# Two attention blocks on one core: row-sum reciprocals taken in 128x8 form through DRAM, one range watch at the end, and VectorE in place of GpSimd for the scaling

## The chip, the cores and the metric

The kernel runs on one core of one Trainium2 chip. A core has a matrix engine (TensorE, PE in the profile), a vector engine (VectorE, DVE), an activation engine (ScalarE, ACT), a general engine (GpSimd, POOL) and a queue engine (SyncE, SP) that here only issues DMAs. Each works through its own instructions in order and waits on semaphores for the others. The metric is the device time of one execution in microseconds; lower is better. Three runs of the kernel before took 2831.9, 2832.25 and 2833.12 us: median 2832.25 us.

## The reference

The input x is eight images (B = 8) of 512 channels by 32x32 = 1024 tokens, in f32. Two attention blocks follow one another:

```python
# layer 0: 8 heads of 64 channels, GroupNorm(32)
h = group_norm(x); q, k, v = per head (w_qkv @ h + b_qkv)
weight = softmax(q.k / sqrt(64), over s);  a = weight @ v
x = x + w_proj @ a + b_proj
# layer 1: one head of 512 channels, GroupNorm(8)
xn = group_norm(x); attn = softmax(q.k / sqrt(512)); out = attn @ v
x = x + p_w @ out + p_b
```

Softmax is a row of exponentials divided by its sum. This kernel takes the exponentials without subtracting a maximum and multiplies the finished product by the reciprocal of each sum. So that this is safe, it keeps a watch over all reciprocals: if one is outside 1e-20 to 1e20, a slow general path recomputes everything at the end. With the inputs here the general path does not run.

## The kernel before, in words

The outer loop goes over the images, b = 0 to 7. In each turn the layer-0 attention of image b is followed by its output projection, then by the layer-1 scores, z product and values of image b-1, then by the layer-0 v, k and q products of the next image. The products are Strassen-Winograd forms ("wino", "conv2", "inner_steps"), which put sums and differences on VectorE and GpSimd.

**A stretch.** `attention0` (L617) goes through 8 stretches per image: 4 pairs of heads, times 2 halves of the 1024 tokens. In a stretch TensorE makes the scores of 8 token blocks (`sc`), ScalarE takes their exponentials (L635, 128x1024 each), and VectorE adds the 8 results into `total` (L637 once, L639 six times). TensorE then multiplies the exponentials by v (`av`), and at once, in `reciprocals` (L588), forms the row sums from `total` with a matrix of ones: 4 products into a PSUM tile `sums`, 128x256, in which each sum stands 32 times. Then TensorE begins the scores of the next stretch. ScalarE copies `av` out to `a` (L653).

**The reciprocals.** VectorE takes the reciprocal of the whole 128x256 `sums` from PSUM (L599), keeps a running minimum (`low_recs`, L600), and GpSimd a running sum (`all_recs`, L601). Four partitions of the result go to DRAM as 4 KB (`rows`, L603) and are read back broadcast over the partitions as `r` (L613 in layer 0, 2 reads of 128 KB; L608 in layer 1, 2 reads of 256 KB). In layer 0, GpSimd multiplies `a` by `r` (L658) for 7 of 8 stretches; in the last one VectorE does, at a later place (L660), and the DMAs go by ScalarE's queue in place of SP's. Layer 1 calls `reciprocals` once per image, in a hook near the end of the z product, and `values1` (L757, L760) multiplies by `r`. In all there are 72 calls: 64 in layer 0 and 8 in layer 1.

**What sets the order.** TensorE's instructions are pinned in program order (L66 to L70). The others are placed by a list scheduler, which works with its own estimates when it builds the program: an instruction takes its place in its engine's queue when the scheduler believes its inputs to be there, the earlier one in the program first. On the chip the queue runs in that fixed order. `keep_in_program_order` pins an instruction behind the one traced just before it on its engine. `extra` is a list of small pieces of work (weight sums, image sums, GroupNorm of the next layer) that is emptied before and after the `av` products of each stretch, and most of its VectorE pieces are pinned (L1045, L285, L286). Each attention needs `a` of its last two stretches in the image sums that open the projection (`steps`, `image_factors`). The loads of x for the projection are issued during the last stretch (L209).

**Buffers.** Large tiles share a pool of 32 (`big`), `sums` and `av` share two PSUM banks (`acc`), `rc` and `r` have two buffers each.

**The end.** After the last image, L1113 reduces `low_recs` and `all_recs` over their columns, L1114 compares with the limits, L1116 multiplies the two answers, a 1x1 product counts over the partitions, and L1119 writes the flag that every engine loads before the branch to the general path.

Of the kernel before, what the change touches and what calls it, by code (L numbers as in the profile page):

```python
# [9 lines left out]
F32 = mybir.dt.float32  # L10
I32 = mybir.dt.int32
AF = mybir.ActivationFunctionType
ALU = mybir.AluOpType
AX = mybir.AxisListType

P = 128
# [6 lines left out]
RECIPROCALS_MIN, RECIPROCALS_MAX = 1e-20, 1e20  # L23
# [6 lines left out]
def two_attention_blocks_kernel(  # L30
# [8 lines left out]
    nc = tc.nc  # L39
    B, C, T = x.shape  # L40
    KC = C // P
# [3 lines left out]
    const = ctx.enter_context(tc.tile_pool(name="const", bufs=1))  # L45
    small = ctx.enter_context(tc.tile_pool(name="small", bufs=3))
# [9 lines left out]
    nc.vector.memset(ones, 1.0)  # L56
    mhalf = const.tile([P, KC], F32, name="mhalf")
    nc.vector.memset(mhalf, -0.5)

    low_recs = const.tile([P, 2, P], F32, name="low_recs")  # L60
    nc.vector.memset(low_recs, 1.0)
    all_recs = const.tile([P, 2, P], F32, name="all_recs")
    nc.gpsimd.memset(all_recs, 0.0)


    def matmul(*args, **kw):  # L66
        tc.keep_in_program_order(nc.tensor.matmul(*args, **kw))  # L67
# [16 lines left out]
    dram = ctx.enter_context(tc.tile_pool(name="dram", bufs=1, space=bass.MemoryType.DRAM))  # L84
# [91 lines left out]
    def main_path(ctx):  # L176
# [2 lines left out]
        upool = ctx.enter_context(tc.tile_pool(name="upool", bufs=1))  # L179
        rpool = ctx.enter_context(tc.tile_pool(name="rpool", bufs=2))  # L180
        rowpool = ctx.enter_context(tc.tile_pool(name="rows", bufs=3, space=bass.MemoryType.DRAM))
        spool = ctx.enter_context(tc.tile_pool(name="spill", bufs=2, space=bass.MemoryType.DRAM))
        ps_acc = ctx.enter_context(tc.tile_pool(name="ps_acc", bufs=2, space=bass.MemoryType.PSUM))

        def big_tile(name, shape=(P, T)):
            return big.tile(list(shape), F32, tag="big", name=name)

        def pair_tile(name):
            return big_tile(name, (P, 2, HT))

        def acc_tile(name):
            return ps_acc.tile([P, HT], F32, tag="acc", name=name)
# [392 lines left out]
            return out  # L585


        def reciprocals(total, uid, across, queue=nc.sync):  # L588

            sums = acc_tile(f"sums_{uid}")[:, : 2 * P].rearrange("p (a b) -> p a b", a=2)
            for i in range(4):
                matmul(sums[ts(i, 32), :, :], ones[:, :32], total[:, :, ts(i, P)], start=True, stop=True)
            rc = rpool.tile([P, 2, P], F32, tag="rc", name=f"rc_{uid}")
            nc.vector.reciprocal(rc, sums)  # L599
            nc.vector.tensor_tensor(low_recs, low_recs, rc, ALU.min)  # L600
            nc.gpsimd.tensor_tensor(all_recs, all_recs, rc, ALU.add)  # L601
            rows = rowpool.tile([2, 4, P], F32, tag="rows", name=f"rows_{uid}")
            queue.dma_start(rows.rearrange("j i n -> i j n"), rc[0:P:32, :, :])  # L603
            if across:
                r = pair_tile(f"r_{uid}")
                for j in range(2):
                    row = rows[j : j + 1].rearrange("j i n -> j (i n)")
                    queue.dma_start(r[:, j, :], row.to_broadcast([P, HT]))  # L608
            else:
                r = rpool.tile([P, HT], F32, tag="r", name=f"r_{uid}")  # L610
                for j in range(2):
                    row = rows[j : j + 1].rearrange("j i n -> j (i n)")
                    queue.dma_start(r[ts(j, 64), :], row.to_broadcast([64, HT]))  # L613
            return r


        def attention0(b, q, k, v, a, extra):  # L617
            n = 0

            for hp in range(KC):  # L620
                for tb in (0, 1) if hp < KC - 1 else (1, 0):
                    uid = f"0_{b}_{hp}_{tb}"
                    total = pair_tile(f"sum_{uid}")
                    es = []
                    for s in range(NS):

                        sc = ps_pools[(0, 2, 1)[n % 3]].tile([P, 2, HT], F32, tag="sc", name=f"sc_{uid}_{s}")
                        n += 1
                        for j in range(2):
                            matmul(  # L630
                                sc[:, j, :], k[hp][ts(j, 64), ts(s, P)], q[hp][ts(j, 64), ts(tb, HT)],
                                start=True, stop=True,
                            )
                        e = pair_tile(f"e_{uid}_{s}")
                        nc.scalar.activation(e, sc, AF.Exp, scale=(C // 8) ** -0.5)  # L635
                        if s == 1:
                            nc.vector.tensor_add(total, es[0], e)  # L637
                        elif s > 1:
                            nc.vector.tensor_add(total, total, e)  # L639
                        es.append(e)  # L640
                    for f in extra.pop(0) if extra else ():
                        f()
                    av = acc_tile(f"av_{uid}")
                    for s in range(NS):
                        for j in range(2):
                            matmul(
                                av[ts(j, 64), :], v(s, 2 * hp + j),
                                es[s][:, j, :], start=(s == 0), stop=(s == NS - 1),
                            )
                    for f in extra.pop(0) if extra else ():  # L650
                        f()
                    dst = a[hp][:, ts(tb, HT)]
                    nc.scalar.copy(dst, av)  # L653

                    last = (hp, tb) == (KC - 1, 0)
                    r = reciprocals(total, uid, False, nc.scalar if last else nc.sync)
                    if not last:
                        nc.gpsimd.tensor_tensor(dst, dst, r, ALU.mult)  # L658
                    else:
                        scaled = lambda dst=dst, r=r: tc.keep_in_program_order(nc.vector.tensor_mul(dst, dst, r))  # L660

            assert not extra
            return scaled


        def scores1(f, gf, gsteps, first, uid, stats):
# [362 lines left out]
        for b in range(B):  # L1029
            extra = [[] for _ in range(2 * 2 * KC)]  # L1030
# [17 lines left out]
            if b > 0:  # L1048
                hf, t = image_factors(h, f"h1_{b - 1}", here)
                for i, fs in enumerate((t[:1], t[1:2], (t[2], t[4]), (t[6], t[3]), (t[5], t[7]), steps[:2], steps[2:4])):  # L1050
                    extra[2 * i + 3] += fs
            elif B > 1:
                hf, t = image_factors(h, "h0_1", here)
# [3 lines left out]
            scaled = attention0(b, q, k, v, a, extra)  # L1057
# [47 lines left out]
        finish()  # L1105


        good = small.tile([P, 2], F32, tag="good", name="good")
        for i, (t, op, limit, within) in enumerate(
            ((low_recs, ALU.min, RECIPROCALS_MIN, ALU.is_ge), (all_recs, ALU.add, RECIPROCALS_MAX, ALU.is_le))  # L1110
        ):
            extreme = small.tile([P, 1], F32, tag="extreme", name=f"extreme{i}")
            nc.vector.tensor_reduce(extreme, t, AX.XY, op)  # L1113
            nc.vector.tensor_scalar(good[:, i : i + 1], extreme, limit, None, within)  # L1114
        both = small.tile([P, 1], F32, tag="both", name="both")
        nc.vector.tensor_mul(both, good[:, 0:1], good[:, 1:2])  # L1116
# [184 lines left out]
```

## Time and profile before

| What | Value |
|---|---|
| median of three runs | 2832.25 us |
| the profiled execution | 2831.03 us, of which its span is 2829.2 us |
| granted TensorE clock | 0.999 |
| TensorE, VectorE, ScalarE, GpSimd busy | 2811.2, 2119.0, 942.7, 1250.6 us |
| reciprocal, 128x256 (L599) | 72 times, mean 1756 ns |
| running minimum (L600), running sum (L601) | 72 times each, mean 438 and 887 ns |
| scaling on GpSimd (L658), on VectorE (L660) | 56 times, mean 2051 ns; 8 times, mean 682 ns |
| sum of exponentials (L639) | 384 times, mean 1351 ns |
| copy `a` (L653), 128x512 | 64 times, mean 585 ns |

One execution was recorded by the hardware profiler. Its page gives the busy time of each engine, the chain of waits that ended last, and groups of instructions. A timeline lists instructions in order of time, several of a kind merged into one row: start, time in us, engine, line, operation, output and inputs, count, and in brackets how long the engine stood idle before it and what ended the wait. "SPq" rows are DMAs being issued by SyncE's queue. The views of waits say, for each engine, what it waited for, in total.

### The profile page before, as it was taken

What the parts mean: (1) busy time and instruction counts of PE and PEld (TensorE: products, weight loads), DVE (VectorE), ACT (ScalarE), POOL (GpSimd) and SP (SyncE); (2) the same over time, 40 slices, a digit from 0 to 9 for tenths busy, and PEclk for the clock granted to TensorE, in tenths of its full rate; (3) what the DMA queues carried; (4) which work ended last, traced back from release to release, by engine and by line L of the source; (5) the groups of instructions that cost most, each with busy time, mean ns of one, the idle gap of its engine ahead of it and who ended that gap; (6) DMA issues with size and microseconds to landing.
All of it is one profiled execution on the core that took longest, in us unless ns stands there. A gap on an engine that the chain in (4) does not pass through costs nothing.

```text
span 2829.2 us, 33980 instructions
## 1 busy us (share of the span) xinstructions
PE 2811.2 (99%) x12434; PEld 1691.7 (60%) x12434; DVE 2119.0 (75%) x2877; ACT 942.7 (33%) x1205; POOL 1250.6 (44%) x1249
## 2 busy tenths in 40 slices
PE   9999999999999999999999999999999999999998
PEld 5435635866367653677537674376843868338584
DVE  5588687766877778777787667877678776887765
ACT  1252452214522145221552215422154312633130
POOL 2214215842267421674117731277223772147672
PEclk9999999999999999999999999999999999999999
DMA  8634403043031330323212232123311224112301
GB/s 286 210 114 147 151 19 121 26 178 138 20 139 53 146 129 23 131 99 119 110 49 105 101 141 90 49 102 123 139 70 49 102 112 158 35 53 95 119 5 68
DMA packets 98850, 291.68 MB, mean 103 GB/s; under 512 B 10803, under 2 KB 42867, under 8 KB 88950
## 3 DMA queue, kind: packets, MB, share of 16 engines
q1 hardware_dynamic: 96886, 287.16, 28.3%
q10 hardware_dynamic: 1792, 2.29, 0.3%
q8 instruction: 100, 1.64, 0.2%
q14 instruction: 72, 0.59, 0.1%
HBM read 236.94 MB, written 52.47 MB: 102 GB/s over the span
## 4 chain that ended last, share of the span: by engine, by line
PE 97%; DVE 1%; issue 1%; POOL 0%; ACT 0%; DVEq 0%; POOLq 0%
PE sc L67 16%; PE av L67 16%; PE psb_av L67 6%; PE psb L67 5%; PE psa_av L67 4%; PE psc_av L67 4%; PE psc L67 3%; PE psa L67 3%; PE psb_z L67 3%; PE psb_p L67 3%; PE psb_k L67 3%; PE psb_g L67 3%; PE psb_v L67 3%; PE psb_q L67 2%; PE psa_p L67 2%; PE psa_z L67 2%
## 5 line engine op out<-in xcount | busy, mean ns | idle before, releaser
L639 DVE TENSOR_TENSOR sum<-sum,e 128x1024 f32<-128x1024 f32 x384 | 518.9, 1351 | 40.7 <-ACT e L635 0.9
L635 ACT ACTIVATE e<-sc 128x1024 f32<-128x1024 f32 x512 | 476.0, 1054 | 79.1 <-PE sc L67 79.1
L67 PE MATMUL sc<-q,k 64*128 64x512 f32 x2048 | 456.8, 596 | 0.0
L67 PE MATMUL av<-e,v 128*64 128x512 f32 x2048 | 453.6, 595 | 0.0
L67 PEld LDWEIGHTS sc<-q,k 64*128 64x128 f32 x2048 | 191.6, 186 | 238.5 <-ACT e L635 109.2
L67 PEld LDWEIGHTS av<-e,v 128*64 128x64 f32 x2048 | 141.4, 137 | 304.3 <-issue 304.3
L601 POOL TENSOR_TENSOR all_recs<-all_recs,rc 128x256 f32<-128x256 f32 x72 | 63.8, 887 | 541.3 <-DVE rc L599 541.3
L658 POOL TENSOR_TENSOR a<-a,r 128x512 f32<-128x512 f32 x56 | 114.9, 2051 | 261.7 <-DMA r<-rows 245.5
L599 DVE RECIPROCAL rc<-sums 128x256 f32<-128x256 f32 x72 | 126.5, 1756 | 46.7 <-PE sums L67 25.3
L653 ACT COPY a<-av 128x512 f32<-128x512 f32 x64 | 37.4, 585 | 321.9 <-PE av L67 321.9
L637 DVE TENSOR_TENSOR sum<-e,e 128x1024 f32<-128x1024 f32 x64 | 78.8, 1231 | 57.0 <-ACT e L635 57.0
L67 PE MATMUL psb<-inner,inner_h 128*128 128x256 f32 x448 | 116.1, 382 | 0.8
L67 PE MATMUL psa_av<-e,z 128*128 128x512 f32 x256 | 113.3, 595 | 0.0
L416 POOL TENSOR_TENSOR inner_h<-h,inner_h 128x256 f32<-128x256 f32 x120 | 107.5, 897 | 3.4
L140 ACT ACTIVATE h<-h,b,s 128x1024 f32<-128x1024 f32 x62 | 78.5, 1270 | 88.0 <-DMA h<-in_x 70.4
L67 PEld LDWEIGHTS psb<-inner,inner_h 128*128 128x128 f32 x448 | 83.9, 190 | 16.6 <-POOL inner L431 3.5
L464 ACT COPY psb_v<-psa_v 128x512 f32<-128x512 f32 (+1 forms) x28 | 14.5, 517 | 227.0 <-DVE o L759 144.6
L416 POOL TENSOR_TENSOR inner_h<-h 128x256 f32<-128x256 f32 x60 | 55.6, 926 | 77.4 <-ACT h L140 77.4
L699 POOL TENSOR_TENSOR sum<-sum,e 128x1024 f32<-128x1024 f32 x32 | 76.1, 2378 | 27.1 <-ACT e L695 25.9
L67 PE MATMUL psb_g<-inner_h,w_m 128*128 128x256 f32 x336 | 85.9, 383 | 0.3
L685 DVE TENSOR_TENSOR e<-psc,u 128x512 f32<-128x512 f32 x56 | 38.7, 691 | 59.0 <-PE psc L67 58.6
L537 POOL TENSOR_TENSOR v<-v,v 128x256 f32<-128x256 f32 x28 | 20.0, 726 | 141.8 <-DVE u_v L532 141.8
(361 smaller groups left out, 5749.6 us busy)
## 6 DMA issues: line engine op xcount, KB each, us to landing
x<-in_x SPq DMA_DIRECT2D x36, 512.0 KB
h<-in_x SPq DMA_DIRECT2D x32, 512.0 KB
spill<-x SPq DMA_DIRECT2D x32, 512.0 KB
h<-spill SPq DMA_DIRECT2D x32, 512.0 KB
x<-spill SPq DMA_DIRECT2D x32, 512.0 KB
out<-x SPq DMA_DIRECT2D x64, 256.0 KB
w_p<-sums_p SPq DMA_DIRECT2D x8, 1792.0 KB
r<-rows SPq DMA_DIRECT2D x112, 128.0 KB
```

The costliest lines, as they stand in the source:

```text
L67: tc.keep_in_program_order(nc.tensor.matmul(*args, **kw))
L140: tc.keep_in_program_order(nc.scalar.activation(dst, src, AF.Identity, bias=b, scale=s))
L416: pin(nc.gpsimd.tensor_tensor(dst, x, y, ALU.subtract))
L599: nc.vector.reciprocal(rc, sums)
L601: nc.gpsimd.tensor_tensor(all_recs, all_recs, rc, ALU.add)
L635: nc.scalar.activation(e, sc, AF.Exp, scale=(C // 8) ** -0.5)
L637: nc.vector.tensor_add(total, es[0], e)
L639: nc.vector.tensor_add(total, total, e)
L653: nc.scalar.copy(dst, av)
L658: nc.gpsimd.tensor_tensor(dst, dst, r, ALU.mult)
L685: nc.vector.tensor_add(dst[0], ps, x[0])
L699: on = lambda dst, x, y: lambda: tc.keep_in_program_order(nc.gpsimd.tensor_tensor(dst, x, y, ALU.add))
```

## The change

- The two running accumulators `low_recs` and `all_recs`, with their 72 updates each on VectorE and GpSimd, are gone.
- In 64 of the 72 calls (7 of 8 stretches, and layer 1) ScalarE copies `sums` to SBUF (`line`); the raw sums go to DRAM (4 KB), come back as a 128x8 tile (`cols`), VectorE takes the reciprocal of that tile, the result goes to DRAM again, into the call's own place in `all_rows`, and from there the broadcast read goes on as before. In the 8 calls of the last stretches (`direct`) VectorE takes the reciprocal of the 128x256 tile as before.
- GpSimd's multiplication is gone. VectorE scales each stretch one stretch later, after the `av` products of the next, ahead of the pieces in `extra`, pinned behind what was traced before it on VectorE.
- At the end all 72 x 1024 reciprocals are loaded as one tile of 128x576, and the two reductions run over it.

```diff
-        def reciprocals(total, uid, across, queue=nc.sync):
+        def reciprocals(total, uid, across, direct=False):
...
-            rc = rpool.tile([P, 2, P], F32, tag="rc", name=f"rc_{uid}")
-            nc.vector.reciprocal(rc, sums)
-            nc.vector.tensor_tensor(low_recs, low_recs, rc, ALU.min)
-            nc.gpsimd.tensor_tensor(all_recs, all_recs, rc, ALU.add)
-            rows = rowpool.tile([2, 4, P], F32, tag="rows", name=f"rows_{uid}")
-            queue.dma_start(rows.rearrange("j i n -> i j n"), rc[0:P:32, :, :])
+            rows = all_rows[len(taken)]
+            taken.append(uid)
+            line = rpool.tile([P, 2, P], F32, tag="line", name=f"line_{uid}")
+            queue = nc.scalar if direct else nc.sync
+            if direct:
+                nc.vector.reciprocal(line, sums)
+                queue.dma_start(rows.rearrange("j i n -> i j n"), line[0:P:32, :, :])
+            else:
+                nc.scalar.copy(line, sums)
+                raw_rows = rowpool.tile([2, 4, P], F32, tag="rows", name=f"rows_{uid}")
+                queue.dma_start(raw_rows.rearrange("j i n -> i j n"), line[0:P:32, :, :])
+                cols = small.tile([P, 8], F32, tag="cols", name=f"cols_{uid}")
+                flat = lambda t: t.rearrange("j i n -> (j i n)").rearrange("(p m) -> p m", p=P)
+                queue.dma_start(cols, flat(raw_rows))
+                recs = small.tile([P, 8], F32, tag="recs", name=f"recs_{uid}")
+                nc.vector.reciprocal(recs, cols)
+                queue.dma_start(flat(rows), recs)
...
-                    for f in extra.pop(0) if extra else ():
+                    for f in [*scaled, *(extra.pop(0) if extra else ())]:
                         f()
                     dst = a[hp][:, ts(tb, HT)]
                     nc.scalar.copy(dst, av)
 
-                    last = (hp, tb) == (KC - 1, 0)
-                    r = reciprocals(total, uid, False, nc.scalar if last else nc.sync)
-                    if not last:
-                        nc.gpsimd.tensor_tensor(dst, dst, r, ALU.mult)
-                    else:
-                        scaled = lambda dst=dst, r=r: tc.keep_in_program_order(nc.vector.tensor_mul(dst, dst, r))
+                    r = reciprocals(total, uid, False, (hp, tb) == (KC - 1, 0))
+                    scaled = [lambda dst=dst, r=r: tc.keep_in_program_order(nc.vector.tensor_mul(dst, dst, r))]
...
+        every = big_tile("every_row", (P, stretches * 8))
+        nc.sync.dma_start(every, all_rows.rearrange("s j i n -> (s j i n)").rearrange("(p m) -> p m", p=P))
         good = small.tile([P, 2], F32, tag="good", name="good")
-        for i, (t, op, limit, within) in enumerate(
-            ((low_recs, ALU.min, RECIPROCALS_MIN, ALU.is_ge), (all_recs, ALU.add, RECIPROCALS_MAX, ALU.is_le))
+        for i, (op, limit, within) in enumerate(
+            ((ALU.min, RECIPROCALS_MIN, ALU.is_ge), (ALU.add, RECIPROCALS_MAX, ALU.is_le))
         ):
             extreme = small.tile([P, 1], F32, tag="extreme", name=f"extreme{i}")
-            nc.vector.tensor_reduce(extreme, t, AX.XY, op)
+            nc.vector.tensor_reduce(extreme, every, AX.X, op)
```

More of the change, by code (lines that the diff above doesn't have):

```diff
@@ L58, in two_attention_blocks_kernel @@
     nc.vector.memset(mhalf, -0.5)
[L60 to L63, printed above, removed]
     def matmul(*args, **kw):
@@ L181, in main_path @@
         rowpool = ctx.enter_context(tc.tile_pool(name="rows", bufs=3, space=bass.MemoryType.DRAM))
+        stretches = B * (2 * KC + 1)
+        all_rows = dram.tile([stretches, 2, 4, P], F32, name="all_rows")
+        taken = []
         spool = ctx.enter_context(tc.tile_pool(name="spill", bufs=2, space=bass.MemoryType.DRAM))
@@ L618, in attention0 @@
             n = 0
+            scaled = []
             for hp in range(KC):
@@ L653, in attention0 @@
                     nc.scalar.copy(dst, av)
-                    last = (hp, tb) == (KC - 1, 0)
-                    r = reciprocals(total, uid, False, nc.scalar if last else nc.sync)
-                    if not last:
-                        nc.gpsimd.tensor_tensor(dst, dst, r, ALU.mult)
-                    else:
-                        scaled = lambda dst=dst, r=r: tc.keep_in_program_order(nc.vector.tensor_mul(dst, dst, r))
+                    r = reciprocals(total, uid, False, (hp, tb) == (KC - 1, 0))
+                    scaled = [lambda dst=dst, r=r: tc.keep_in_program_order(nc.vector.tensor_mul(dst, dst, r))]
             assert not extra
-            return scaled
+            return scaled[0]
         def scores1(f, gf, gsteps, first, uid, stats):
@@ L1105, in main_path @@
         finish()
+        assert len(taken) == stretches
+        every = big_tile("every_row", (P, stretches * 8))
+        nc.sync.dma_start(every, all_rows.rearrange("s j i n -> (s j i n)").rearrange("(p m) -> p m", p=P))
         good = small.tile([P, 2], F32, tag="good", name="good")
-        for i, (t, op, limit, within) in enumerate(
-            ((low_recs, ALU.min, RECIPROCALS_MIN, ALU.is_ge), (all_recs, ALU.add, RECIPROCALS_MAX, ALU.is_le))
+        for i, (op, limit, within) in enumerate(
+            ((ALU.min, RECIPROCALS_MIN, ALU.is_ge), (ALU.add, RECIPROCALS_MAX, ALU.is_le))
         ):
             extreme = small.tile([P, 1], F32, tag="extreme", name=f"extreme{i}")
-            nc.vector.tensor_reduce(extreme, t, AX.XY, op)
+            nc.vector.tensor_reduce(extreme, every, AX.X, op)
             nc.vector.tensor_scalar(good[:, i : i + 1], extreme, limit, None, within)
```

## The prediction

> **What bounds the kernel now.** I read the page first: the busy shares, then the chain of waits that ended last.
>
> ```profile
> PE 2811.2 (99%) x12434; PEld 1691.7 (60%) x12434; DVE 2119.0 (75%) x2877; ACT 942.7 (33%) x1205; POOL 1250.6 (44%) x1249
> PE 97%; DVE 1%; issue 1%; POOL 0%; ACT 0%; DVEq 0%; POOLq 0%
> ```
>
> TensorE is busy 99% of the span, and the chain runs 97% through it. A busy PE need not be a PE at its peak, so I went on to what TensorE waited for in the whole span. All its waits there add up to 8.7 us; the two longest are the load of a weight at the start and one ScalarE copy:
>
> ```profile
> PE tr_wk L70 <- DMA rawk<-in_w: 3.7, 1, 3.7
> PE psb_v L67 <- ACT u_v L454: 1.2, 1, 1.2
> ```
>
> [...]
>
> The change touches VectorE, GpSimd and ScalarE, so it can win at most these 8.7 us, and little of that lies where it works. What it can lose is read from one stretch. These are rows of the timeline from 386 to 404 us, engine by engine:
>
> ```profile
> 388.15 0.64 PE L67 MATMUL sums<-sum,ones 128*32 128x256 f32 x8
> 402.80 0.64 PE L67 MATMUL sums<-sum,ones 128*32 128x256 f32 x8
> 388.91 1.76 DVE L599 RECIPROCAL rc<-sums 128x256 f32<-128x256 f32 x1 [0.40 <-issue]
> 391.86 1.22 DVE L637 TENSOR_TENSOR sum<-e,e 128x1024 f32<-128x1024 f32 x1 [0.74 <-ACT e L635]
> 393.19 8.75 DVE L639 TENSOR_TENSOR sum<-sum,e 128x1024 f32<-128x1024 f32 x6
> 388.26 0.59 ACT L653 COPY a<-av 128x512 f32<-128x512 f32 x1 [4.48 <-PE av L67]
> 389.89 7.44 ACT L635 ACTIVATE e<-sc 128x1024 f32<-128x1024 f32 x8 [1.04 <-PE sc L67]
> 396.02 2.19 POOL L658 TENSOR_TENSOR a<-a,r 128x512 f32<-128x512 f32 x1 [4.30 <-DMA r<-rows]
> 390.69 0.56 SPq L603 DMA_DIRECT2D rows<-rc  x1
> 392.40 1.10 SPq L613 DMA_DIRECT2D r<-rows  x2
> ```
>
> TensorE needs `total` at 402.80; VectorE's seven sums run from 391.86 to 401.94. So the place that decides has 0.86 us to spare, and the sums start when ScalarE has two exponentials, not when the reciprocal is done: VectorE stands idle 0.74 us before them. A faster reciprocal moves nothing here.
>
> **Part 1, VectorE's and GpSimd's work.** Gone: 64 of the 72 reciprocals at 1.76 us, 72 minima at 0.44, on GpSimd 72 sums at 0.89 (63.8 us) and 56 scalings at 2.05 (114.9). New on VectorE: 56 scalings at 0.68 (the row of L660, same shape) and 64 reciprocals of 128x8. No row has that shape; it lies between 0.06 (1756 ns by 8/256 columns) and 0.20 (the aggregation of 128x12), and I take 0.15, near the 128x4 copy. VectorE: -112.6 - 31.5 + 38.1 + 9.6 = -96 us. GpSimd's scaling also stretches one VectorE sum beside it: six sums take 8.75 here, but 7.87 in the row at 138.57, where no scaling runs beside them. So each stretch gains another 0.88, and the slack at 402.80 becomes 0.86 + 0.88 = 1.74 us. On the path: 0, since TensorE waits for none of this.
>
> **Part 2, ScalarE's copy.** 64 copies of 128x256 out of PSUM, 0.36 each (the 128x256 form of L464 has a mean of 357 ns). In the stretch it follows the copy of `a`: 388.85 to 389.21. Queued behind it are the eight exponentials; the first starts at 389.89, when its scores are there, so 0.68 us cover it. Without that cover a delay would go into the chain of sums, which has 1.74. Path: 0.
>
> **Part 3, the two extra trips, and the wait they put into VectorE's queue.** SP issues 2 more DMAs per call; on its queue they stand ahead of the next loads. The write of 4 KB takes 1.71 us (390.69 to 392.40, where the read that waits for it is issued). The raw sums go out at 389.2 and land at 390.9. The read into 128x8 has no row: from below it is a write of the same 4 KB, 1.71; from above one of the two reads of 128 KB, which take 3.62 together (392.40 to 396.02), less half of the 1.10 they take to issue, 3.07. I take 1.71, the row of the same size; `cols` is there at 392.65, at most at 394.0.
>
> The new reciprocal waits for it in VectorE's queue, with the sums of the next stretch behind it, and behind those TensorE's `sums`. If the scheduler puts it behind the first or second sum (ending 393.1 and 394.5), it costs its 0.15. If it stands ahead of the first, the sums shift by 392.65 + 0.15 - 391.86 = 0.94, still inside 1.74. At the upper bound the shift is 2.28 and TensorE loses 0.54 per stretch. Path, by the value taken: 0.
>
> The rest follows: written back by 394.65 + 1.71 = 396.4, `r` broadcast by 400.0. The scaling stands behind the sums, which now end at 401.06: 1.1 us early, and it may be 3 us late before the next sums, which cannot begin until 406.5.
>
> [...]
>
> **Part 4, the first attention, where the queues are full.** In the first two stretches the write took 4.38 and 7.06 us and `r` came 8.5 and 6.8 us after its issue:
>
> ```profile
> 134.41 0.33 SPq L291 DMA_DIRECT2D sums_p<-prepare_p  x1
> 136.20 0.61 SPq L603 DMA_DIRECT2D rows<-rc  x1
> 140.16 0.33 SPq L333 DMA_DIRECT2D w_p<-sums_p  x1
> 140.58 1.62 SPq L613 DMA_DIRECT2D r<-rows  x2
> ```
>
> They stand behind 1.8 MB stores and loads of weights. There only GpSimd waited; now VectorE will. The raw sums land at about 140.2, behind `sums_p`. If `cols` is issued ahead of `w_p`, it is there at 141.9; if behind, at about 147 (the two `r` reads behind it served GpSimd at 149.08). With the reciprocal behind the second sum (139.9) and five sums of 1.33 after it, the sums end at 148.7 or 153.8; TensorE wants them at 148.2. Loss 0.5 or 5.6, and 0 if the reciprocal stands behind all the sums. The second stretch could pay as much again: 0 to 11 in all. No row tells which order SP gets; I take the middle of 0.5 and 5.6, **3 us**, once.
>
> **Part 5, ends of attentions, layer 1, end of the kernel.** The seventh stretch's `r` now comes about 4 us later, while 2 MB of x are issued at 437.65. They are drained by 446 (410 GB/s from 442 to 444 us, 18 after 446); behind them `r` lands near 450 (446 + 3.6) instead of 441. Then follow scaling and two image sums on VectorE, 2.0 us, to 452; TensorE wants them at 454.30. Path 0, but only 2 us of cover, in each of 8 attentions. In layer 1 the sums are formed at 2766.07 and VectorE first uses `r` at 2784.08; before, the reciprocal waited until 2768.37 for its turn. The steps (0.4 + 1.7 + at most 3.1 + 0.2 + 1.7, and some 4 for `r` with twice the bytes) make 11 us and fit. At the end the load of all reciprocals (295 KB) can go when SP is idle (2774.9 to 2785.6). The two reductions take 0.95 each (0.42 by 576/256), and TensorE's last product stays behind its other work. If the load stands behind the last store of the output instead, at 2824.05, then 3.07 and about 2.4 of VectorE bring the flag to 2830 in place of 2822.5: +7 or so. Between 0 and 7, I take **1 us**, nearer to 0 because SP is idle earlier.
>
> **Sum.** 2831.03 (the profiled execution) + 0 + 0 + 0 + 3 + 1 = 2835.0. The median of the runs shown is 1.2 above that execution: **2836 us**, 0.13% over 2832.25. A measurement of this kernel can tell about 0.2%, 5.7 us, from no change.
>
> **The rivals.**
> - *A. The full queues cost their upper bound* (11 in the first attention, or 7 at the end): 2840 to 2847. For it: the rows of 4.38 and 7.06. Against: the same traffic then drains while TensorE stands. Chance 0.22.
> - *B, slower: VectorE blocked in every stretch.* The new reciprocal stands ahead of the sums and `cols` lands after about 393.4 (391.86 + 1.74 - 0.15). At 394.0: 0.54 x 56 = 30 us, 2866. For it: the order is fixed by an estimate, and GpSimd's row shows 4.3 us of waiting for `r`. Against: the scheduler must believe in two trips done in 2.6 us. Chance 0.12.
> - *C, slower: the end of each attention.* If the seventh `r` is late by another 2 to 4 us, 8 x 1 to 2 us: 2844 to 2852. Chance 0.12.
> - *D, faster: VectorE's relief reaches TensorE.* All of TensorE's waits gone would be 2823.5; by over 0.2% needs 5.7 of the 8.7 us. Against: 3.7 of them are a load at the start. Chance 0.04.
> - That the change relieves VectorE but not the time is the forecast itself, 0.50.
>
> **How the numbers follow.** Same 0.50; slower A + B + C = 0.46; faster 0.04. The forecast alone spans 2831 to 2838. The range reaches over A and C and nearly all of B: 2831 to 2864.
>
> **What the new profile would show.** VectorE near 1980 us (2119 - 96, less 0.88 in some 50 stretches), GpSimd near 1072, ScalarE near 966. In a later stretch seven sums of about 1.23 and TensorE without a gap at `sums`; TensorE's waits should name VectorE's sums only between 119 and 180 us. Wrong would be a wait of VectorE for `cols` in each stretch that TensorE's `sums` wait for too, or a flag written after 2830.

## The result, and the profile after

The changed kernel takes 2840.24 us (median of 12 runs, 2837.97 to 2846.22) against 2832.10 us for the kernel before (12 runs, 2831.52 to 2833.12). The ratio is 1.0030, 95% interval 1.0021 to 1.0039: slower by 0.3%. The time lies inside the predicted range, above the forecast of 2836, whose own band ended at 2838, and at the lower end of what rival A gave (2840 to 2847). The spread of the runs has grown from 1.6 to 8.2 us.

The profiled execution took 2841.53 us, with a span of 2839.7 us against 2829.2. From its page, the busy line and the chain by engine:

```profile
PE 2813.3 (99%) x12434; PEld 1693.3 (60%) x12434; DVE 1973.0 (69%) x2860; ACT 966.8 (34%) x1269; POOL 1113.7 (39%) x1120
PE 89%; DVE 6%; DMA 2%; issue 1%; ACT 1%; SPq 0%; DVEq 0%; ACTq 0%
```

VectorE lost 146 us of work and GpSimd 137, and the chain, which was 97% TensorE, now runs 6% through VectorE and 2% through DMAs (shares of the way that the chain takes, not of the time lost). Work that was hidden went away, and waits on the path came in its place. What TensorE waits for in the whole span (us in total, times, longest):

```profile
PE sums L62 <- DVE sum L649: 6.6, 9, 2.5
PE psb_av L62 <- DVE u_av L236: 3.1, 3, 1.1
PE psb_v L62 <- ACT u_v L452: 0.6, 1, 0.6
```

The first two lines are new; the third stood at 1.2.

TensorE executes the same 12434 weight loads in the same order in both traces. So the start of each can be compared with the start of the same one before, and the delay added up stage by stage. This is an ordinary table, made from the two traces:

| stage | delay gained, us |
|---|---|
| up to the first attention | +0.25 |
| first attention, stretches 1 to 7 | +6.38 |
| projection behind it (240 to 300 us) | -1.47 |
| eighth stretch of the seven later attentions | 7 x 0.36 to 0.38 = +2.55 |
| values of layer 1, eight images | +2.91 |
| all else, the end of the kernel included | -0.15 |
| sum | +10.47 |

This execution lies 1.3 us over the median of its runs, and the profiled one of before 1.1 us under its own; 10.5 less these is the 8.1 us between the medians.

**A later stretch** looks as predicted. From the timeline, 393 to 409 us, engine by engine:

```profile
394.40 0.57 SPq L606 DMA_DIRECT2D rows<-line  x1
396.12 0.32 SPq L609 DMA_DIRECT2D cols<-rows  x1
397.01 1.23 DVE L647 TENSOR_TENSOR sum<-e,e 128x1024 f32<-128x1024 f32 x1 [3.65 <-ACT e L645]
398.15 0.20 DVE L611 RECIPROCAL recs<-cols 128x8 f32<-128x8 f32 x1
398.34 7.88 DVE L649 TENSOR_TENSOR sum<-sum,e 128x1024 f32<-128x1024 f32 x6
394.00 0.37 ACT L604 COPY line<-sums 128x256 f32<-128x256 f32 x1
407.95 0.64 PE L62 MATMUL sums<-sum,ones 128*32 128x256 f32 x8
```

The write of the raw sums takes 1.72 us (394.40 to 396.12), the reciprocal stands behind the first sum and starts with no wait, and the seven sums end at 406.22, 1.74 us before TensorE needs them.

**The first attention** does not. SP, VectorE and TensorE, 134 to 171 us:

```profile
135.08 0.62 SPq L606 DMA_DIRECT2D rows<-line  x1
141.20 0.33 SPq L331 DMA_DIRECT2D w_p<-sums_p  x1
141.62 0.38 SPq L609 DMA_DIRECT2D cols<-rows  x1
138.82 5.21 DVE L649 TENSOR_TENSOR sum<-sum,e 128x1024 f32<-128x1024 f32 x4
148.28 0.20 DVE L611 RECIPROCAL recs<-cols 128x8 f32<-128x8 f32 x1 [4.25 <-DMA cols<-rows]
148.40 2.51 DVE L649 TENSOR_TENSOR sum<-sum,e 128x1024 f32<-128x1024 f32 x2
166.77 0.20 DVE L611 RECIPROCAL recs<-cols 128x8 f32<-128x8 f32 x1 [3.02 <-DMA cols<-rows]
150.97 0.64 PE L62 MATMUL sums<-sum,ones 128*32 128x256 f32 x8 [2.47 <-DVE sum L649]
151.54 8.83 PE L62 MATMUL sc<-q,k 64*128 64x512 f32 x32
169.46 0.64 PE L62 MATMUL sums<-sum,ones 128*32 128x256 f32 x8 [2.07 <-DVE sum L649]
```

Read it from the bottom: TensorE waits for the last of VectorE's sums; that sum stood behind the reciprocal; the reciprocal waited 4.25 us for `cols`, whose load SP issued at 141.62, right behind the load of `w_p` at 141.20. It came 6.66 us after its issue; in the later stretch above it took at most 2.03 (396.12 to 398.15). That the 1.8 MB load ahead of it is the reason is read from the order and these times: no run here issues `cols` ahead of `w_p`. There is a second cost. The scores after the first wait take 8.83 us where the same 32 matmuls take 7.14 elsewhere. The view by windows of 2 us gives the cause in its ninth number, the granted TensorE clock:

```profile
150.00:152.00 2.00, 1.03 (x10) 0.46 (x12) 1.97 (x3) 0.33 (x1) 0.00 (x0) 1.00 0.71 288
152.00:154.00 2.00, 2.00 (x8) 0.92 (x6) 1.44 (x3) 0.93 (x2) 0.00 (x0) 0.53 0.01 0
154.00:156.00 2.00, 2.00 (x8) 0.75 (x8) 0.00 (x0) 1.17 (x2) 0.00 (x0) 0.62 0.90 288
```

(Columns: window, its length, busy time with count of PE, weight loads, DVE, ACT and POOL, then the clock, the DMA share and GB/s.) The clock was at half from 152.1 to 155.5 us, which loses 2 x 0.47 + 2 x 0.38 = 1.7 us of full clock. It did not fall after the second wait (1.00 from 168 to 174 us).

**The eighth stretch** of the second attention, 437 to 453 us:

```profile
437.42 0.73 POOL L414 TENSOR_TENSOR inner_h<-h 128x256 f32<-128x256 f32 x1 [102.90 <-PE av L62]
441.09 1.70 POOL L414 TENSOR_TENSOR inner_h<-t_h,inner_h 128x256 f32<-128x256 f32 x1
442.31 9.91 DVE L649 TENSOR_TENSOR sum<-sum,e 128x1024 f32<-128x1024 f32 x6
452.27 0.64 PE L62 MATMUL sums<-sum,ones 128*32 128x256 f32 x8 [0.29 <-DVE sum L649]
```

GpSimd's subtractions for the next convolution began at 450.23 before, behind its last scaling and accumulation:

```profile
450.23 1.17 POOL L416 TENSOR_TENSOR inner_h<-h 128x256 f32<-128x256 f32 x1
```

Nothing is ahead of them now, so they begin 12.8 us earlier (18 us earlier against TensorE's work, which comes 5.15 us later here) and run beside VectorE's sums. Both become slower: a subtraction takes 1.70 us in place of the 0.73 of the first ones, while VectorE rests, and six sums 9.91 in place of 7.88. The stretch of 2.03 is more than the slack of 1.74.

### The profile page after: what moved, and what is told of

It reads as the page before. It is cut to its first block, busy times and chain, and to the rows that moved or that the text cites. A ratio compares the mean times of both kernels' runs of the same rounds, so it can differ in the third digit from the quotient of the medians.

```text
span 2839.7 us, 34004 instructions
## 1 busy us (share of the span) xinstructions
PE 2813.3 (99%) x12434; PEld 1693.3 (60%) x12434; DVE 1973.0 (69%) x2860; ACT 966.8 (34%) x1269; POOL 1113.7 (39%) x1120
## 4 chain that ended last, share of the span: by engine, by line
PE 89%; DVE 6%; DMA 2%; issue 1%; ACT 1%; SPq 0%; DVEq 0%; ACTq 0%
PE sc L62 14%; PE av L62 13%; PE psb L62 5%; PE psb_av L62 5%; PE psa_av L62 3%; PE psa L62 3%; PE psc L62 3%; PE psc_av L62 3%; DVE sum L649 3%; PE psb_z L62 3%; PE psb_k L62 3%; PE psb_g L62 3%; PE psb_v L62 3%; PE psb_p L62 3%; PE psb_q L62 2%; PE psa_z L62 2%
## 5 line engine op out<-in xcount | busy, mean ns | idle before, releaser
L649 DVE TENSOR_TENSOR sum<-sum,e 128x1024 f32<-128x1024 f32 x384 | 485.6, 1264 | 35.2 <-DVE sum L649 0.9
L414 POOL TENSOR_TENSOR inner_h<-h,inner_h 128x256 f32<-128x256 f32 x120 | 117.1, 977 | 3.5
L414 POOL TENSOR_TENSOR inner_h<-t_h 128x256 f32<-128x256 f32 x90 | 103.2, 1153 | 28.2 <-issue 20.3
L535 POOL TENSOR_TENSOR g<-g,g 128x256 f32<-128x256 f32 x32 | 23.0, 729 | 184.0 <-DVE u_g L530 184.0
L414 POOL TENSOR_TENSOR inner_h<-t_h,inner_h 128x256 f32<-128x256 f32 x90 | 90.8, 1009 | 2.4
L701 ACT ACTIVATE e<-e 128x1024 f32<-128x1024 f32 x64 | 65.8, 1054 | 48.7 <-DVE e L691 26.2
L62 PEld LDWEIGHTS psa_av<-e,z 128*128 128x128 f32 x256 | 48.0, 190 | 57.3 <-issue 56.9
```

Of the source, the lines that this page charges most:

```text
L414: pin(nc.gpsimd.tensor_tensor(dst, x, y, ALU.subtract))
L535: nc.gpsimd.tensor_tensor(d, x, y, ALU.add)
L701: nc.scalar.activation(e[c, cc, r], e[c, cc, r], AF.Exp, scale=scale)
```

## The experiments

The theory after this comparison was: the loss has three places (the wait for `cols` in the first attention, GpSimd's early subtractions, the values of layer 1), and each can be undone by itself. The rivals put the loss on the later scaling, or on the extra trips as such. Each time is a median with its ratio to the kernel before, run side by side on one chip.

### The first two stretches direct

```diff
+        EARLY = ("0_0_0_0", "0_0_0_1")
-            if direct:
+            if direct or uid in EARLY:
                 nc.vector.reciprocal(line, sums)
```

> The changed kernel, but the first two stretches of the first attention take their reciprocals straight from the sums in 128x256 form on VectorE, with one trip through DRAM, so no VectorE instruction there waits for a transfer. Nothing is left out. Theory (the wait for cols in full queues costs 4.5 us and sets off a clock drop that costs 1.7 more): TensorE's two waits of 2.47 and 2.07 us at the sums of the first attention are gone, the granted clock stays at 1.0 there, and the time falls by about 6.4 us, from 2840 to some 2834. What is left over before (about +4) sits in the eighth stretches and in layer 1's values. Rival (it is VectorE's later scaling, waiting for r in the same queues, that holds up the sums): scalings still wait for r in the second and third stretch, TensorE still waits 2 us or more, and the time stays within 2 us of 2840.

2833.49 us, ratio 1.0009 (1.0000 to 1.0018). The first attention loses 0.00 us, the clock stays at 1.00 (from 146 to 160 and from 164 to 174 us), and the eighth stretches keep their loss (2.57). The theory holds; the later scaling is in this kernel too and costs the first attention nothing.

### Only the scaling moved

The kernel before, with this edit alone:

```diff
-                    for f in extra.pop(0) if extra else ():
+                    for f in [*scaled, *(extra.pop(0) if extra else ())]:
...
-                    if not last:
-                        nc.gpsimd.tensor_tensor(dst, dst, r, ALU.mult)
-                    else:
-                        scaled = lambda ...
+                    scaled = [lambda dst=dst, r=r: tc.keep_in_program_order(nc.vector.tensor_mul(dst, dst, r))]
...
-            return scaled
+            return scaled[0]
```

> The kernel before with one part of the change alone: VectorE scales, a stretch later, in place of GpSimd; reciprocals in 128x256 form, one trip, minima and accumulation as before. Nothing is left out. Theory (GpSimd, relieved of the scalings, starts its subtractions for the next layer inside the eighth stretch and slows VectorE's sums there): the subtractions stand in the eighth stretch, its six sums take about 9.9 us in place of 8.8, and TensorE waits 0.2 to 0.5 us at the sums of the later attentions, some 2 to 3 us in all; the first attention loses under 1 us; layer 1's values lose nothing: 2834 to 2835. Rival (the 128x8 form and its wait are what makes the eighth stretch late): the eighth stretches lose nothing here and the time is that of before, 2832, or up to 2 us less, because the sums of the other stretches are shorter.

2832.94 us, ratio 1.0004 (0.9995 to 1.0013). The first attention and the eighth stretches lose 0.00: my theory, as put there, fell. The timeline of this kernel says why:

```profile
451.32 0.90 POOL L601 TENSOR_TENSOR all_recs<-all_recs,rc 128x256 f32<-128x256 f32 x1 [13.76 <-PE psa_p L67]
452.19 1.17 POOL L416 TENSOR_TENSOR inner_h<-h 128x256 f32<-128x256 f32 x1
```

The accumulation that this kernel keeps stands in GpSimd's queue ahead of the subtractions and holds them until after the eighth stretch. In the kernels here they are let go only when scaling and accumulation have both left GpSimd: with the watch alone, or with the scaling back on GpSimd, the eighth stretches lose 0.00 too. The part of the rival that puts the time at that of before is what was measured; its reason, the 128x8 form, is tested next.

### The seventh stretch's scaling back on GpSimd

```diff
+                    if (hp, tb) == (KC - 1, 1):
+                        nc.gpsimd.tensor_tensor(dst, dst, r, ALU.mult)
+                        scaled = []
+                    else:
                         scaled = [lambda dst=dst, r=r: ...]
```

> The changed kernel, but in each attention the scaling of the seventh stretch alone goes back to GpSimd, right behind its reciprocals, so that GpSimd's subtractions for the next layer stand behind it in the queue. Nothing is left out. Theory: the subtractions start after the eighth stretch as before, its six sums take 8.8 us or less, TensorE's waits of 0.26 to 0.51 us there are gone, the time falls by 2 to 2.6 us to about 2838, and the first attention keeps its loss of 6.4. If the b=0 projection gained its 1.6 us because the subtractions came early, that gain goes too and the time stays near 2839.5. Rival (the eighth stretch is late because cols or r of the seventh lands late): the waits stay.

2836.85 us, ratio 1.0019 (1.0010 to 1.0028). The eighth stretches lose 0.00. The rows of the same place in this kernel:

```profile
447.61 1.38 POOL L667 TENSOR_TENSOR a<-a,r 128x512 f32<-128x512 f32 x1 [112.76 <-DMA r<-all_rows]
448.95 1.71 POOL L414 TENSOR_TENSOR inner_h<-h 128x256 f32<-128x256 f32 x1
442.64 9.10 DVE L649 TENSOR_TENSOR sum<-sum,e 128x1024 f32<-128x1024 f32 x6
```

One instruction that waits for `r` holds the queue until 448.95, and six sums take 9.10 us in place of 9.91, which the slack of 1.74 covers. `cols` and `r` land no earlier than in the changed kernel, so it was the early subtractions. The first attention keeps its loss (6.03).

### Layer 1 direct

```diff
-            if direct:
+            if direct or across:
                 nc.vector.reciprocal(line, sums)
```

> The changed kernel, but the eight calls of layer 1 take their reciprocals straight from the sums in 128x256 form with one trip; layer 0 keeps the 128x8 form. Nothing is left out. Theory (in layer 1 r comes about 6 us later over three trips, so the scheduler puts the first product with r ahead of the image sums of z instead of behind the first, VectorE waits for r with these sums queued behind it, and TensorE then waits about 1.1 us for u_av in some images): the waits at psb_av go, about 3 us in all, to 2837. Rival (the waits come from VectorE being late for another reason, the loss is a matter of one profiled execution): they stay and the time stays within 1 us of 2840.

2838.79 us, ratio 1.0026 (1.0016 to 1.0037). In the profiled execution the values of layer 1 lose 0.15 us in place of 2.91, which fits the theory. By medians the loss falls from 8.1 to 7.0 us, less than the theory's 3. And six other kernels here that keep the 128x8 form in layer 1 lose 0.73, 0.74, 0.71, -0.27, -0.41 and -0.18 us there in their profiled executions, while of five further ones that do not have it there three (the three edits together, the watch alone, the scaling held later) lose 0.78, 0.85 and 0.92, and two 0.18 and -0.03. So the 2.9 was in good part of that one execution, as the rival said, and what the form costs layer 1 in a typical run is not settled. The spread of runs hints at more in some executions: with the form in layer 1 the runs of the changed kernel and of four experiments span 8.2, 8.2, 7.5, 9.0 and 4.7 us, and without it 3.7, 1.2, 1.5 and 3.0. (Two kernels with the form in layer 1 and the reciprocal pinned first are left out, with 6 and 4 runs only; they span 1.5 and 12.3.) No profile fell on one of the long executions, so this is a hint and not shown.

### The first two parts without the later scaling

The changed kernel, with GpSimd scaling the first seven stretches as before; the edit is the one above with the condition `(hp, tb) != (KC - 1, 0)`.

> The change without its third part: 128x8 form over two trips and the one watch at the end, but GpSimd scales the first seven stretches right behind their reciprocals, as before. Nothing is left out. Theory (three places): in the eighth stretches GpSimd's subtractions stand behind its scaling, so the 2.3 us there are gone; the first attention keeps its two waits for cols, 4.5 to 6.4 us; layer 1's values keep their 3: 2837 to 2839. VectorE's sums beside a scaling are 0.9 us longer per stretch, inside the slack. Rival (the later scaling on VectorE is what costs the first attention its time): 2833 or less.

2838.80 us, ratio 1.0022 (1.0013 to 1.0031). The first attention loses 7.54 us (waits of 2.55 and 3.16 us at the sums, and 1.83 more, near the 1.7 of one half clock), the eighth stretches 0.00, the values of layer 1 only 0.71. The rival falls: VectorE scales nothing there in this kernel, and the loss stays.

### The three edits together

> The changed kernel with the three edits of the first experiments together: reciprocals straight from the sums in the first two stretches and in layer 1, and the seventh stretch's scaling on GpSimd; 53 stretches of layer 0 keep the 128x8 form. Nothing is left out. Theory (the three places are independent and hold the whole loss): the profiled executions gave back 6.5, 3.1 and about 2.3 us one at a time, together 11.9 of the 10.5 us lost, less about 1 us of the gain in the b=0 projection that goes when GpSimd's subtractions start late again: 2831 to 2832.5, the same as before within 0.1%, no TensorE wait at the sums over 0.1 us and none at psb_av. Rival (the three losses hide one another, or a fourth place is late): 2834 or more.

2831.10 us, ratio 0.9997 (0.9988 to 1.0006), in runs that span 1.2 us. No wait at the sums is left in the list of TensorE's waits; one of 0.5 us at `psb_av` is, which the theory had excluded and the kernel with the watch alone has too. The three edits account for the whole loss. They do not simply add up: by medians they give back 6.5, 3.1 and 1.2 us one at a time, 10.7, and 8.9 together (the first two figures in the text above are such differences of medians).

### The reciprocal behind the sums

The first two stretches keep the 128x8 form and its trips; only the reciprocal is put later.

```diff
+                if uid in EARLY:
+                    def rest():
+                        tc.keep_in_program_order(nc.vector.reciprocal(recs, cols))
+                        queue.dma_start(flat(rows), recs)
...
+                    return r, rest
...
+                            if s == NS - 1 and b == 0 and hp < 2:
+                                tc.keep_in_program_order(add)
...
-                    scaled = [lambda dst=dst, r=r: ...]
+                    scaled, carry = (carry + [*rest], [scale]) if rest else (carry + [scale], [])
```

> The changed kernel with the 128x8 form and both extra trips kept everywhere, but in the first two stretches VectorE's reciprocal is put behind all seven sums of the next stretch (it stood behind the fifth), and the scaling one stretch later still. Nothing is left out. Theory (not the trips cost the time but the place in VectorE's queue where their end is waited for): TensorE's waits of 2.5 and 2.1 us at the first attention's sums and the half clock after the first are gone though cols lands as late as before; the time falls by about 6.4 to some 2834. Rival 1 (the transfers in the full queues hold up something else, the weights loaded there): the loss stays in part, 2837 or more. Rival 2: the later scalings now stand before the third stretch's sums and wait for r, so TensorE waits there in their place, 2 us or more.

2835.66 us, ratio 1.0014 (1.0005 to 1.0023). Both theory and rival 2 are right in part. The two waits and the half clock are gone; one wait came in their place, in the fourth stretch:

```profile
172.25 0.20 DVE L624 RECIPROCAL recs<-cols 128x8 f32<-128x8 f32 x1 [3.78 <-DMA cols<-rows]
180.25 0.64 PE L62 MATMUL sums<-sum,ones 128*32 128x256 f32 x8 [2.00 <-DVE sum L663]
```

The `cols` of the third stretch is late because SP came to its write late: the `r` of the second, issued at 167.06 and waiting for a write of its own, stood ahead of it. The first attention loses 2.07 in place of 6.38. So the place of the wait decides, and SP's queue passes a delay on.

### The reciprocal ahead of the first sum, and one trip more

On top of the first experiment, rival B's case made by hand: in the 54 stretches that use the form, the reciprocal is pinned ahead of all seven sums, and in the second kernel one more trip of 4 KB is added.

```diff
-                nc.vector.reciprocal(recs, cols)
+                rec = nc.vector.reciprocal(recs, cols)
+                if not across:
+                    tc.keep_in_program_order(rec)
...
-                            nc.vector.tensor_add(total, es[0], e)
+                            tc.keep_in_program_order(nc.vector.tensor_add(total, es[0], e))
...
 # second kernel only, ahead of the load of cols
+                if not across:
+                    again = rowpool.tile([2, 4, P], F32, tag="again", name=f"again_{uid}")
+                    queue.dma_start(again, raw_rows)
+                    raw_rows = again
```

> The changed kernel with the first two stretches direct, so that their wait is out of the picture; in the other 54 stretches of layer 0 that use the 128x8 form VectorE's reciprocal is pinned ahead of the first sum of the next stretch instead of behind it. Nothing is left out. Theory (slack of 1.74 us at the sums): the sums start when the reciprocal ends, about 1.4 us later (cols lands about 2.1 us after its issue at 396.1, the sums stood at 397.0), the slack falls to some 0.5 us, TensorE waits nowhere more than before: within 1 us of the run with the first two stretches direct, 2833.5. Rival (cols lands later than 2.6 us after its issue in many stretches, and the slack is used up): 0.5 us or more in each of 54 stretches, 27 us or more.

2841.44 us, ratio 1.0032 (1.0020 to 1.0045), which neither side expected. In the other stretches the reciprocal costs some 0.67 of the slack (1.74 becomes about 1.07) and nothing of the time, but for one that loses 0.87. Each eighth stretch of the later attentions loses 1.0 to 1.6 us, 10.07 together (the first one's loses 0.42):

```profile
436.14 1.70 DVE L651 TENSOR_TENSOR sum<-e,e 128x1024 f32<-128x1024 f32 x1
437.94 9.90 DVE L653 TENSOR_TENSOR sum<-sum,e 128x1024 f32<-128x1024 f32 x6
447.90 0.64 PE L62 MATMUL sums<-sum,ones 128*32 128x256 f32 x8 [1.48 <-DVE sum L653]
```

Here the subtractions stretch all seven sums, by 2.5 us together, and 2.5 less 1.07 of slack is the wait. Two costs, of which one fits the slack alone and the other nearly does, were spent from the same slack.

> As the kernel with the reciprocal pinned ahead of the first sum, with one more trip of 4 KB through DRAM ahead of the load of cols in each of the 54 stretches. Nothing is left out. Theory (the wait costs time from the point where it passes the slack): the trip adds 1.7 to 2.2 us, the slack of about 0.5 us is passed by 1.2 to 1.7, and TensorE waits as much at the sums of each of 54 stretches: 65 to 92 us, 2900 to 2925. If such a wait also halves the granted clock, as the one of 2.47 us did and the one of 2.07 us did not, up to 1.7 us more for each, 2990 or more; waits under 2 us should leave the clock at 1.0. Rival (the wait is covered by other work of TensorE): no loss in most stretches, under 2840.

2917.87 us, ratio 1.0309 (1.0294 to 1.0325), inside the theory's 2900 to 2925. TensorE's waits:

```profile
PE sums L62 <- DVE sum L657: 70.2, 54, 3.4
```

Most stretches lose 0.9 to 1.0 us, which with the 1.07 of slack makes the trip 1.9 to 2.0, an estimate; the eighth ones of the later attentions lose 3.4. The theory had 1.2 to 1.7 in each of the 54, so its mechanism holds and its sum came out by other terms: most stretches cost less, because the slack was 1.07 and not 0.5, and the eighth ones and the half clocks (a mean granted clock of 0.996 over 2910.3 us, against 0.999 before: some 9 us by these two) cost more. Past the slack every stretch pays, and nothing else of TensorE's covers it.

### The reciprocal first, with the three edits

> The kernel with all three edits, and the reciprocal of 128x8 pinned ahead of the first sum in the 53 stretches that use it. Nothing is left out. Theory (in the run with the reciprocal first, the eighth stretches alone were late, by 0.6 to 1.8 us each, because a shift of 0.7 and seven sums stretched by 2.6 us together passed the slack of 1.74): with GpSimd's subtractions held back the shift of 0.7 fits alone, no TensorE wait at the sums, 2831 to 2832. Rival (the late reciprocal by itself costs the eighth stretches): 2835 or more.

2835.10 us, ratio 1.0013 (1.0004 to 1.0022): the rival's number. The eighth stretches of the later attentions still lose 0.20 to 0.61 us each, 2.65 in all; the first one's loses 0.31 and one other stretch 0.60. From the second attention:

```profile
441.99 2.01 POOL L669 TENSOR_TENSOR a<-a,r 128x512 f32<-128x512 f32 x1 [112.82 <-DMA r<-all_rows]
437.65 9.10 DVE L651 TENSOR_TENSOR sum<-sum,e 128x1024 f32<-128x1024 f32 x6
```

With the subtractions held back, GpSimd's scaling and the first subtraction still stretch two of the six sums, to 2.11 and 1.56 us, 1.2 together, over 1.07 of slack. I had counted only the shift of 0.67 and left out what the holding instruction costs itself.

### The watch alone, and the scaling held from the second attention on

The first is the kernel before with the accumulators gone and the one watch at the end; the second is the kernel with the three edits, its GpSimd scaling given the further condition `and b > 0`.

> The kernel before with the one watch over all reciprocals at the end and without the minima on VectorE and the accumulation on GpSimd; reciprocals in 128x256 form and scaling on GpSimd as before. Nothing is left out. Theory (no TensorE wait names this work, and GpSimd's scaling of the seventh stretch still holds the subtractions back): 2831.3 to 2832.5, the same. The load of all reciprocals and two reductions of 0.74 us at the end cost nothing. Rival (the end of the kernel pays for the late load): 2 to 7 us more.

2829.97 us, ratio 0.9992 (0.9983 to 1.0001): the same, though 1.3 us under the band that the theory gave. The end of the kernel pays nothing, so the rival falls.

> The kernel with all three edits, but the seventh stretch's scaling goes to GpSimd only from the second attention on; in the first, GpSimd's subtractions may start early. Nothing is left out. Theory (the early start costs nothing in the first attention, where the eighth stretch ended with 0.72 us of slack, and gave 1.6 us back in the projection behind it, of which holding kept about 0.7): 1 us less than with all three edits, 2830.1. Rival: the same 2831.1 within 0.3 us, if VectorE's work in the projection and not GpSimd's decides there.

2830.85 us, ratio 0.9995 (0.9986 to 1.0004), 0.25 us under the kernel with three edits: the rival. The projection behind the first attention gains 0.81 us here and 1.28 there, the other way round from my theory. It gains in every kernel without the accumulators, 1.25 us in the one with the watch alone, where GpSimd still scales, and not in the kernel with the scaling alone, which keeps them (+1.57, a half clock in it included: 0.71, 0.50 and 0.93 from 266 to 272 us). So the gain goes with the accumulators that left VectorE and GpSimd, not with early subtractions.

Three kernels have medians 0.7 to 2.0 us below that of the kernel before (watch alone, three edits, held later). All three intervals reach 1.0, so none is shown to be faster.

## Why the prediction was right or wrong

**What bounds the kernel** was right: with the new waits taken away, the time is that of before, though VectorE has 129 us less to do (1990 in the kernel with three edits).

**Part 1** held. The slack is 1.74, to the hundredth, and VectorE's 1973 us are near the 1980 given. GpSimd has 1114 in place of 1072: its subtractions now run beside VectorE's sums and take longer (1.70 us in place of 0.73 in the rows above). I priced that contention for the scaling that went, and did not ask what GpSimd would do next. **Part 2** held: 0.37 us a copy, and no delay.

**Part 3** held by the value taken. The write takes 1.72 us against 1.71, the order is reciprocal behind first sum, and later stretches lose nothing but in the eighth. The bound that I kept for rival B (0.54 us a stretch) was a fair warning: with the reciprocal first, 1.07 us of slack were left, and one more trip made the profiled span 79 us longer than that of the first experiment.

**Part 4** is the term that was mis-sized: 3 us taken, "once", 6.4 measured, inside the 0 to 11 that it gave. Its mechanism was right: VectorE waited for `cols`, which SP had issued behind `w_p`. Two numbers of its later case were off, one against the other: `cols` was there at 148.3, for which I had said "about 147", and the reciprocal stood behind the fifth sum, not the second. Behind the second, the late `cols` would have cost some 6.6 us by the sum given there (148.28 + 0.15 + 5 x 1.33 - 148.50); behind the fifth it cost 2.47, so that a single wait comes near the 3 is luck. Two more things failed in the step. The 3 was taken once, though the second stretch stood behind the same kind of traffic; it paid 2.07 us. And I counted the wait alone, not the half clock that the first wait set off, 1.7 us more.

**Part 5** looked at the right place for the wrong reason. I watched `r` and its 2 us of cover at the ends of the attentions; `r` did land in time. The 2.55 us come from the engine that was relieved: its queue was empty, and it started the next work into VectorE's narrowest stretch. The prediction counted GpSimd's relief as a gain alone, 0.88 us of slack in each stretch. Layer 1 was put at 0 and lost 2.9 in the profiled execution, of which the experiments leave open how much is typical. The end of the kernel was put at 1 and cost nothing: the load of all reciprocals went out at 2785.48, in SP's idle time, as I had expected, and two reductions took 0.74 us each. Two of the signs that I had named came out against me: TensorE's waits name VectorE's sums in seven later eighth stretches too, and the flag was written at 2832.92, after 2830. But that is the 2822.5 of before plus the 10.4 us lost ahead of it, not a cost of the end.

**Not in the sum** was a gain, 1.5 us in the projection, rival D's mechanism on a small scale. **The chances**: the forecast had 0.50 for no change and lost to rival A's time, but by a sum of terms (6.4 + 2.55 + 2.9 - 1.5, in the profiled execution) and not by rival A's one bound. Two of these terms the prediction had put at nothing, so that the sum lands in rival A's bracket is luck; the range held because it was drawn over the rivals.

## What to carry to other kernels

When work leaves an engine that is not the bottleneck, ask two things: which instruction now waits for a transfer at the head of a queue that the bottleneck depends on, and what the relieved engine will start earlier, beside whom. Write down the slack of each stretch once and spend it from one account, because costs that fit one by one do not fit together. Give a wait in the first stretches, where loads fill the queues (a DMA share of 1.06 and 1.02 from 146 to 150 us here), its upper bound for each stretch, and add what the clock may do after it (1.7 us here).

## What the hardware showed that was not expected

**TensorE's granted clock fell to half behind some of its waits and not behind others, and the length of the wait does not tell which.** In the changed kernel's first attention the wait of 2.47 us ended at 150.97, and at 152.1 the clock fell to half; behind the wait of 2.07 us it stayed at 1.00:

```profile
168.00:170.00 2.00, 0.55 (x8) 0.16 (x8) 1.51 (x5) 0.08 (x1) 0.00 (x0) 1.00 0.08 27
170.00:172.00 2.00, 2.00 (x14) 1.03 (x12) 0.05 (x1) 1.17 (x2) 0.00 (x0) 1.00 0.35 115
172.00:174.00 2.00, 2.00 (x14) 0.81 (x10) 1.47 (x2) 2.00 (x4) 0.00 (x0) 1.00 0.05 6
```

In the kernel with one trip more, a wait of 3.37 us left the clock alone, and one of 2.49 us had half a clock behind it. Its TensorE rows, and the clock behind each:

```profile
243.33 1.08 PE L62 MATMUL sums<-sum,ones 128*32 128x256 f32 x8 [2.49 <-DVE sum L657]
463.08 0.64 PE L62 MATMUL sums<-sum,ones 128*32 128x256 f32 x8 [3.37 <-DVE sum L657]
```

```profile
242.00:244.00 2.00, 0.67 (x8) 0.20 (x8) 2.00 (x2) 0.00 (x0) 1.92 (x3) 0.81 0.88 361
244.00:246.00 2.00, 2.00 (x6) 0.84 (x3) 2.00 (x3) 0.00 (x0) 2.00 (x2) 0.50 0.01 4
246.00:248.00 2.00, 2.00 (x5) 0.91 (x4) 2.00 (x2) 0.46 (x1) 1.92 (x3) 0.84 0.00 0
462.00:464.00 2.00, 0.92 (x9) 0.46 (x10) 2.00 (x2) 0.00 (x0) 2.00 (x2) 1.00 0.00 0
464.00:466.00 2.00, 2.00 (x6) 0.85 (x5) 2.00 (x3) 0.27 (x1) 1.92 (x3) 1.00 0.03 8
466.00:468.00 2.00, 2.00 (x6) 0.85 (x5) 2.00 (x2) 0.31 (x1) 2.00 (x3) 1.00 0.00 0
```

The three windows from 242 to 248 us lose 2 x (0.19 + 0.50 + 0.16) = 1.7 us of full clock, as much as the drop in the changed kernel. In the kernel with the scaling alone the clock fell in the projection, at about 266.8 us, where TensorE's longest wait between 248 and 280 us is 1.2 us but it stands idle for 0.84 and 0.96 us of two windows, and 1.7 us were lost again:

```profile
264.00:266.00 2.00, 1.16 (x8) 0.97 (x8) 2.00 (x4) 0.75 (x2) 0.00 (x0) 1.00 1.07 322
266.00:268.00 2.00, 1.04 (x5) 1.04 (x6) 1.71 (x4) 0.91 (x2) 0.00 (x0) 0.71 1.09 366
268.00:270.00 2.00, 2.00 (x11) 2.00 (x11) 0.86 (x2) 0.00 (x0) 0.00 (x0) 0.50 0.96 301
270.00:272.00 2.00, 2.00 (x19) 2.00 (x19) 1.52 (x3) 0.57 (x1) 0.00 (x0) 0.93 0.87 341
```

In the kernel that leaves the scaling on GpSimd, the two waits at the places of 2.47 and 2.07 are longer:

```profile
152.60 0.64 PE L62 MATMUL sums<-sum,ones 128*32 128x256 f32 x8 [2.55 <-DVE sum L649]
170.48 0.64 PE L62 MATMUL sums<-sum,ones 128*32 128x256 f32 x8 [3.16 <-DVE sum L649]
```

Its first attention loses 7.54 us, 1.83 more than the two together. That is about one half clock, so by this estimate one of the two, though longer than 2.47, left the clock alone. What decides beside the length is not shown. If a wait at the same place halves the clock in one execution and not in another, 1.7 us come and go with it. That can be a part of the wider spread of the changed kernel's runs; it was not tested, since each kernel was profiled once.

**GpSimd and VectorE slow each other** in the rows named here, where both run element-wise work on f32: a sum of 1.225 us (at 394.52 before) took 1.56 beside the subtractions (at 442.31 in the changed kernel) and 2.11 beside the scaling (at 397.18 before), and a subtraction (`inner_h<-t_h,inner_h`) 1.70 (at 441.09 in the changed kernel) in place of 0.73 (at 455.12 before).
